# q and k of a transposed attention: seven products for eight, and a third of the depthwise taps on other engines

## The chip, the cores and the metric

The kernel runs on one core of a Trainium2 chip, in fp32 throughout. The metric is the device time of one execution in microseconds. The median of three runs of the kernel before is 2740.94 us (2740.43 to 2743.98).

## The reference, cut to what matters

The input x has 384 channels of 192 x 192 pixels. Layer 0 normalises it over groups of channels, makes q, k and v with a 1x1 convolution (384 to 1152 channels), pools 2x2 by the maximum, and applies a depthwise 3x3 convolution. q and k then only enter as their norms and as q k^T per head (48 x 48 a head), summed over all 96 x 96 pooled pixels. Layer 1 is a depthwise 7x7 convolution over the whole image.

```python
def _L0_conv_ref(x, w_qkv, b_qkv, w_dw, b_dw, w_proj, b_proj, temperature, a1, a2, a3, a4):
    ...
    qkv = jnp.einsum('bchw,oc->bohw', x, w_qkv) + b_qkv[None, :, None, None]
    hs, ws = (h // DS, w // DS)
    qkv = qkv.reshape(b, 3 * c, hs, DS, ws, DS).max(axis=(3, 5))
    qkv = lax.conv_general_dilated(qkv, w_dw, (1, 1), 'SAME', feature_group_count=3 * c, dimension_numbers=('NCHW', 'OIHW', 'NCHW'))
    qkv = qkv + b_dw[None, :, None, None]
    q, k, v = jnp.split(qkv, 3, axis=1)
    ...
    q = q / jnp.clip(jnp.linalg.norm(q, axis=-1, keepdims=True), 1e-12)
    k = k / jnp.clip(jnp.linalg.norm(k, axis=-1, keepdims=True), 1e-12)
    attn = jnp.einsum('bhcn,bhdn->bhcd', q, k) * temperature[None]
    ...
x = x + _L0_conv_ref(_gn(x), ...)
x = x + _L1_conv_ref(_gn(x), L1_conv_weight)
```

## The kernel before

The 384 channels lie on 128 partitions in three tiles (KT = 3); q and k together have six output tiles (ct = 0 to 5). The image is cut into 24 blocks (NB) of eight image rows, which are four pooled rows (PR) of 96 pixels (PS). The stages follow each other in this order:

- Statistics: x is read once; VectorE takes its moments. The first three blocks stay in on-chip memory (`held`), and as soon as two of the three channel tiles are normalised, TensorE begins the sums of blocks 0 and 1 (`begin`); ScalarE puts 20 of these begun sums aside (`spots`, in `rowbuf` and `more`).
- q and k, the stage that the change is in: a loop over b from 0 to 24. For each block and output tile, `pooled` runs three groups of 512 columns; a group is three matrix products (one a channel tile) into a bank of PSUM, and one VectorE reduction from there (L672), which takes the maximum of 2x2 and writes the pooled pixels into a `ring` of 14 rows per output tile. `bordered` copies the ring's wrap-around rows on ScalarE (L697, L701). One block later `depthwise` makes the nine taps of an output tile on VectorE (one scaled copy, L712, and eight multiply-adds, L717) into `qk`. `finish` turns the result in blocks of 32 x 32 on VectorE (L781), squares and sums it on ScalarE (L729), and after three output tiles 16 ScalarE copies (L735) finish the turning. `products` then adds 12 matrix products of the turned q and k to `grams` (L751), two blocks behind.
- v, the attention and the projection; then layer 1, whose matrices `weights` has meanwhile laid out on GpSimd (L578 to L605): one piece a block, from block 0 on.

The sums of q and k use a pool of four one-bank tiles of PSUM (`pq`), and a pool of three (`ptr`) takes small sums and the squares' unused output; `grams` has a bank of its own. The order of the instructions on an engine is mostly the program's own: from block 2 on `pinned` (and `keep`) hold each engine's instructions in the order in which they are written, and put gram products between the others.

An fp32 matrix product is two instructions on TensorE in the trace, each with a load of weights. The waits between engines are set by the recording layer from the tiles that the instructions read and write. The block of x is loaded by `load_x` on SyncE's queue into one of three buffers.

```python
    ptr = psx.enter_context(tc.tile_pool(name="ptr", bufs=3, space=PSUM))
    ...
    pq = qx.enter_context(tc.tile_pool(name="pq", bufs=4, space=PSUM))
    ...
                for kt in range(KT) if begun is None else (TWO,):
                    ins = nc.tensor.matmul(
                        ps,
                        wq[:, kt, ct * P : (ct + 1) * P],
                        rows[:, kt, :, g * 64 : (g + 1) * 64],
```

Of the kernel before, what the change touches and what calls it, by code (L numbers as in the profile page):

```python
# [13 lines left out]
P = 128  # L14
# [72 lines left out]
def conv_preact_d2(  # L87
# [184 lines left out]
    ptr = psx.enter_context(tc.tile_pool(name="ptr", bufs=3, space=PSUM))  # L272
    qx = ExitStack()
    pq = qx.enter_context(tc.tile_pool(name="pq", bufs=4, space=PSUM))
# [20 lines left out]
    with tc.tile_pool(name="stp", bufs=1) as stp, tc.tile_pool(name="xsp", bufs=5) as xsp:  # L295
# [29 lines left out]
        def total(name, n, terms):  # L325

            ps = ptr.tile([P, C], F32, name=name, tag="tr")
            for i, (lhs, rhs) in enumerate(terms):
                keep(
                    nc.tensor.matmul(  # L330
                        ps[:, 0:n], lhs, rhs, start=(i == 0), stop=(i == len(terms) - 1)
                    )
                )
            return ps[:, 0:n]
# [87 lines left out]
        def begin(i):  # L422
            b, ct, g = begun_qk[i]
            ps = pq.tile([P, 512], F32, name=f"pq{b}_{ct}_{g}_begun", tag="pq")
# [46 lines left out]
        bias_ps = ptr.tile([P, C], F32, name="bias_ps", tag="tr")  # L471
# [91 lines left out]
    with ExitStack() as bx:  # L563
# [6 lines left out]
        def weights(kt, i0, i1):  # L570
# [7 lines left out]
            nc.gpsimd.memset(g, 0.0)  # L578
            for kr in range(KS):
                lo, hi = max(i0, kr), min(i1, kr + TR)  # L580
                if lo < hi:
                    nc.gpsimd.tensor_copy(
                        bass.AP(
                            g.tensor,
                            g.offset + ((lo - i0) * GQ + CP - 1) * TR + lo - kr,
                            [g.ap[0], [TR, KS], [GQ * TR + 1, hi - lo]],
                        ),
                        w7s[:, kt, kr, :].unsqueeze(2).to_broadcast([P, KS, hi - lo]),
                    )
            lo, hi = max(i0, HALO), min(i1, HALO + TR)  # L590
            cs = slice(kt * P, (kt + 1) * P)
            for v in range(CP if lo < hi else 0):
                nc.gpsimd.dma_start(
# [6 lines left out]
                )  # L600
            for i in range(i0, i1):
# [3 lines left out]
                nc.gpsimd.dma_start(  # L605
# [6 lines left out]
                )  # L612
# [22 lines left out]
        ring = []  # L635
        for ct in range(2 * KT):
            ring.append(padp.tile([P, 3 * PR + 2, PS + 2], F32, name=f"ring{ct}"))
# [11 lines left out]
        def pooled(b, ct, xb, taps):  # L649
# [4 lines left out]
            for g in range(3):  # L654
                begun, there = sums_qk.pop((b, ct, g), (None, False))
                ps = begun
                if not there:
                    ps = pq.tile([P, 512], F32, name=f"pq{b}_{ct}_{g}", tag="pq")
# [44 lines left out]
        def depthwise(b, ct, dst, pin):  # L703

            r0 = b % 3 * PR
            for tap in range(9):
# [3 lines left out]
                if tap == 0:  # L710
                    pin(
                        nc.vector.tensor_scalar(  # L712
                            dst, src, w, bdb[:, ct : ct + 1], ALU.mult, ALU.add
                        )
                    )
                else:
                    pin(nc.vector.scalar_tensor_tensor(dst, src, w, dst, ALU.mult, ALU.add))  # L717
# [8 lines left out]
        def squares(b, ct, t):  # L726

            junk = ptr.tile([P, C], F32, name=f"junk{b}_{ct}", tag="tr")
            nc.scalar.activation(junk, t, AF.Square, accum_out=ssq[:, ct, b : b + 1])  # L729

        def turned(side, turns):

            for a in range(P // Q):
                for f in range(P // Q):
                    nc.scalar.copy(  # L735
                        side[f * Q : (f + 1) * Q].rearrange("p c (t n) -> p t c n", n=P)[
                            :, :, :, a * Q : (a + 1) * Q
                        ],
                        turns[a * Q : (a + 1) * Q].rearrange("p t (c n) -> p t c n", n=P)[
                            :, :, :, f * Q : (f + 1) * Q  # L740
                        ],
                    )
                yield
# [23 lines left out]
        copies, sides = iter(()), []  # L767
        turns = multiplied = None
# [4 lines left out]
        def finish(b, ct, dst, taps, now=False):  # L773

            nonlocal copies, turns
            some(taps, 9)
            s, t = divmod(ct, KT)
            if t == 0:
                turns = trp.tile([P, KT, PB], F32, name=f"turns{b}_{s}", tag=f"turns{s}")
            flat = dst.rearrange("p h w -> p (h w)")  # L780
            ins = nc.vector.transpose(turns[:, t], flat)  # L781
            if b > 0:
                pinned(ins)

            for _ in copies:
                pass
            squares(b, ct, flat)
            if t == KT - 1:
                side = trp.tile(
                    [P, PB // P, C], F32, name=f"qkT{b}_{s}", tag=f"qkT{s}", bufs=2 - s  # L790
                )
                sides.append(side)
                copies = turned(side, turns)
                for _ in range(4 if now else 2):
                    next(copies)
# [20 lines left out]

        last = None
        for b in range(NB + 1):
            xb, xvb = None, []
            if b < NB:  # L820
                xb = held.pop(b) if b in held else load_x(b, "xq")
            else:

                qx.close()
                pv = psx.enter_context(tc.tile_pool(name="pv", bufs=2, space=PSUM))
                for n in range(3):
                    t = xpool.tile([P, 2, UT, KT, RB * HW], F32, name=f"xv_begun{n}", tag="xb")
                    for k in range(2):
                        i, t0 = divmod((2 * n + k) * UT, NT)
                        for kt in range(KT):  # L830
                            nc.sync.dma_start(t[:, k, :, kt], image_rows(kt, order[i], t0, UT))
                        xvb += [(i, t0, ct, t[:, k]) for ct in range(KT)]
            for ct in range(2 * KT):
                dst, taps = None, iter(())
                if b > 0:
                    dst = qkp.tile([P, PR, PS], F32, name=f"qk{b}_{ct}", tag="qk")
                    taps = depthwise(b - 1, ct, dst, pinned if b > 1 else lambda ins: ins)
                if b < NB:
                    if ct == KT + 1 and b > 1:
                        done, sides = sides[0:2], sides[2:]  # L840
                        between.append(products(b - 2, done))
                    if b == 0 and ct < 2:

                        if ct == 0:
                            pooled(b, 0, xb, taps)
                            pooled(b, 1, xb, taps)
                            biases()
                    else:
                        pooled(b, ct, xb, taps)
                    bordered(b, ct)  # L850
# [5 lines left out]
                if b == NB:  # L856
                    if ct == KT - 1:
                        between.append(products(b - 2, sides[0:2]))
                    some(taps, 4)
                    convolve(*xvb.pop(0), pinned)  # L860
                    some(taps, 5)
                    convolve(*xvb.pop(0), pinned)
            if b == NB:
                finish(*last, True)
                for _ in range(2):
                    convolve(*xvb.pop(0), pinned)
                norms()
                for _ in products(b - 1, sides[2:4]):
                    pass
                for args in xvb:  # L870
                    convolve(*args, pe_keep)
            if b == 2:
                for tiles in vrows:
                    row_borders(tiles)
            if b < len(pieces):
                with tc.issue_after(stats0):
                    weights(*pieces[b])
# [793 lines left out]
```

## Time and profile before

| what | value |
|---|---|
| median of three runs | 2740.94 us |
| span of the profiled execution, first to last instruction | 2751.1 us |
| statistics, to the first product of block 0 | about 169.5 us |
| q and k, blocks 0 to 23 on TensorE | about 169.5 to 1302 us |
| last taps of q and k on VectorE | to about 1355 us |
| v, attention, projection, layer 1 | the rest |

The profile is of one execution, which took 10 us more than the median. Busy times of an engine are the union of its instructions; a group's line gives the sum and the mean of one. "Idle before" is the time in which the engine had nothing to run ahead of these instructions, and the name after it is what ended most of that.

### The profile page before, as it was taken

Reading aid. Unit: us, or ns where it says so; the run is one execution under the profiler, and the core shown is the slowest. Engines: PE = TensorE matmul, PEld = TensorE weight load, DVE = VectorE, ACT = ScalarE, POOL = GpSimd, SP = SyncE. Lnnn points to the kernel's source line nnn. Section 1 sums busy time; section 2 is a strip of 40 time slices with the busy share of each in tenths; the row PEclk is TensorE's granted clock in tenths of the full one; section 3 lists DMA queues with packets and bytes.
Section 4 is the critical chain, followed back from the end, with each engine's and each line's share of the span. In section 5 each row is a group of like instructions: output and inputs, shape, how many; then the busy total and the mean of one; then the engine's idle time right before and its main releaser. Section 6 shows DMA issues by size and latency. Waiting matters only on the chain. (4 is left out here: it accounts for less than half of the span.)

```text
span 2751.1 us, 25751 instructions
## 1 busy us (share of the span) xinstructions
PE 2583.4 (94%) x8365; PEld 1527.5 (56%) x8365; DVE 2404.7 (87%) x3538; ACT 1141.3 (41%) x2262; POOL 748.0 (27%) x885
## 2 busy tenths in 40 slices
PE   0399999999999999999989989999998999999998
PEld 0144444444444444444546656666666677777776
DVE  7989999999999999999898979988889788777886
ACT  0043334343334343333302322322324577777776
POOL 1024454100000000000002320100101577777887
PEclk9999999999999999999999999999999899999999
DMA  9976767401010110111136996675755999999998
GB/s 381 401 262 210 245 207 246 146 35 69 35 69 35 37 67 35 69 35 53 69 122 235 342 373 237 212 254 179 240 196 181 339 347 363 365 372 371 368 376 271
DMA packets 234087, 581.01 MB, mean 211 GB/s; under 512 B 16688, under 2 KB 165792, under 8 KB 217184
## 3 DMA queue, kind: packets, MB, share of 16 engines
q1 hardware_dynamic: 173456, 283.44, 29.4%
q0 software_dynamic: 37376, 148.85, 15.7%
q10 hardware_dynamic: 23120, 147.07, 14.2%
q8 instruction: 67, 1.10, 0.2%
q14 instruction: 68, 0.56, 0.1%
HBM read 370.93 MB, written 208.21 MB: 211 GB/s over the span
## 5 line engine op out<-in xcount | busy, mean ns | idle before, releaser
L662 PE MATMUL pq<-xq,wq 128*128 128x512 f32 x2268 | 1021.9, 595 | 0.0
L717 DVE SCALAR_TENSOR_TENSOR qk<-ring,wd,qk 128x384 f32<-128x384 f32 x1152 | 696.3, 615 | 25.1
L662 PEld LDWEIGHTS pq<-xq,wq 128*128 128x128 f32 x2268 | 411.7, 190 | 421.9 <-issue 372.4
L549 PE MATMUL pv<-xv,wq 128*128 128x384 f32 x1512 | 499.2, 490 | 18.1 <-DVE rows L555 9.5
L1575 PE MATMUL pc<-main,w 128*128 128x288 f32 x1536 | 435.0, 405 | 3.5 <-issue 1.3
L1595 DVE TENSOR_SCALAR apart<-pc,rb 32x576 f32<-32x576 f32 x384 | 312.2, 813 | 118.4 <-PE pc L1575 98.3
L549 PEld LDWEIGHTS pv<-xv,wq 128*128 128x128 f32 x1512 | 288.8, 192 | 220.2 <-DVE rows L555 13.2
L1575 PEld LDWEIGHTS pc<-main,w 128*128 128x128 f32 x1536 | 289.8, 189 | 86.8 <-issue 2.9
L1593 ACT ACTIVATE apart<-pc,rb 32x576 f32<-32x576 f32 x384 | 281.4, 733 | 132.8 <-PE pc L1575 128.0
L672 DVE TENSOR_REDUCE ring<-pq 128x128 f32<-128x512 f32 x428 | 290.0, 679 | 52.0 <-PE pq L662 51.2
L735 ACT COPY qkT<-turns 32x288 f32<-32x288 f32 x768 | 329.4, 429 | 12.1 <-DVE turns L781 3.2
L1041 DVE SCALAR_TENSOR_TENSOR vb<-rows,wd,vb 128x576 f32<-128x576 f32 x384 | 313.0, 818 | 10.8
L729 ACT ACTIVATE junk<-qk 128x384 f32<-128x384 f32 x144 | 71.2, 494 | 471.7 <-DVE qk L717 470.8
L1575 PE MATMUL pc<-aux,h 128*128 128x288 f32 x768 | 248.5, 405 | 1.1 <-POOL aux L1510 1.1
L803 POOL TENSOR_TENSOR rn<-rn,halfpos 128x6 f32<-128x6 f32 x1 | 1.4, 1359 | 842.7 <-DVE rn L802 842.7
L1534 POOL COPY res<-apart 128x1152 f32<-128x1152 f32 (+1 forms) x96 | 213.1, 2253 | 62.6 <-DMA out_dram<-res 51.2
L1168 DVE TENSOR_TENSOR sx<-xr,y 128x576 f32<-128x576 f32 x180 | 203.9, 1174 | 21.2 <-ACT y L1139 15.1
L1209 POOL DMA_DIRECT2D sd<-sx x96 | 72.2, 756 | 501.1 <-DVE sx L1168 482.2
L555 DVE TENSOR_REDUCE rows<-pv 128x192 f32<-128x768 f32 x144 | 137.8, 957 | 57.7 <-PE pv L549 57.7
L1575 PEld LDWEIGHTS pc<-aux,h 128*128 128x128 f32 x768 | 144.9, 189 | 42.9 <-POOL aux L1510 1.5
L751 PEld LDWEIGHTS grams<-qkT,qkT 128*96 128x96 f32 x576 | 92.1, 163 | 136.8 <-issue 132.1
L1188 ACT ACTIVATE wq<-sx,negmid 128x1152 f32<-128x1152 f32 x96 | 120.6, 1257 | 107.6 <-DVE sx L1168 103.4
(234 smaller groups left out, 2307.8 us busy)
## 6 DMA issues: line engine op xcount, KB each, us to landing
sd<-sx POOLq DMA_DIRECT2D x96, 600.0 KB, 10.0
out_dram<-res SPq DMA_DIRECT2D x192, 288.0 KB, 10.5
main<-sd ACTq DMA_DIRECT2D x46, 1200.0 KB, 7.0
xr<-in_x_dram SPq DMA_DIRECT2D x45, 1152.0 KB, 12.7
xq<-in_x_dram SPq DMA_DIRECT2D x21, 2304.0 KB, 8.1
xv<-in_x_dram SPq DMA_DIRECT2D x126, 384.0 KB, 6.4
w<-wt ACTq DMA_DIRECT2D x46, 1024.0 KB, 7.0
xs<-in_x_dram SPq DMA_DIRECT2D x24, 1536.0 KB, 15.1
```

What stands on the lines that cost most here:

```text
L549: nc.tensor.matmul(ps[:, u, 0 : RB * HW], wq[:, kt, o : o + P], xb[:, u, kt, :], start=(kt == 0), stop=(kt == KT - 1),)
L555: nc.vector.tensor_reduce(rows[ct][:, 1 + t0 : 1 + t0 + UT, 1 : PS + 1], ps[:, :, 0 : RB * HW].rearrange("p u (a w b) -> p u w a b", a=2, ...
L662: ins = nc.tensor.matmul(ps, wq[:, kt, ct * P : (ct + 1) * P], rows[:, kt, :, g * 64 : (g + 1) * 64], start=(kt == 0), stop=(kt == KT - 1) ...
L672: ins = nc.vector.tensor_reduce(t[:, r0 : r0 + PR, 1 + g * 32 : 1 + (g + 1) * 32], ps.rearrange("p (h a w b) -> p h w a b", h=PR, a=2, b=2 ...
L717: pin(nc.vector.scalar_tensor_tensor(dst, src, w, dst, ALU.mult, ALU.add))
L735: nc.scalar.copy(side[f * Q : (f + 1) * Q].rearrange("p c (t n) -> p t c n", n=P)[:, :, :, a * Q : (a + 1) * Q], turns[a * Q : (a + 1) * Q ...
L1041: pin(nc.vector.scalar_tensor_tensor(dst, src, w, dst, ALU.mult, ALU.add))
L1168: nc.vector.tensor_tensor(bass.AP(flat.tensor, flat.offset + at(e) + a * RUN, [flat.ap[0], [JP, NT], [1, NJ], [at(f) - at(e), 2]],), xq[:, ...
L1534: keep(copy(res[ps, k], apart[ps, :, k].rearrange("p e n -> p n e")))
L1575: nc.tensor.matmul(ahead[q][:, k, 0 : NT * NJ], lhs, rhs, start=(j == 0), stop=(j == 2), skip_group_check=True,)
L1593: keep(nc.scalar.mul(dst, src, scale))
L1595: keep(nc.vector.tensor_scalar_mul(dst, src, scale))
```

## The change

From block 2 on, the products over channel tiles 0 and 1 for a pair of output tiles are made by Strassen's scheme. The two output tiles and the two rows of a pooling pair form a 2 x 2 of blocks, and so do the two channel tiles; seven products of combined operands take the place of eight, and the third channel tile adds four as before. One such group covers a pair of output tiles and half of a block's columns: 384 columns of each operand, in 11 products; a block is six groups, all blocks 132.

- The combinations of weights (`combos`) are made once on GpSimd. The two channel tiles carry different normalisation factors, so `ratio` scales one to the other. The combinations of pixels (`mixes`: T4, T2, T1, T3) are made for each block and half by one ScalarE scaling of 768 columns (`prescaled`) and four GpSimd operations of 384 (`mixed`).
- The sums live in PSUM tiles of three banks: `bank_da` (D, and two banks that take the shared and base products in turn) and `bank_bc` (two banks B in turn, and C). ScalarE copies partial sums from bank to bank, four copies a group. VectorE makes one addition of 768 elements, one maximum of 768 and one of 384 a group, the last into the ring.
- Of the six output tiles' taps, tiles 0 and 3 (`MOVED`) go to `moved`: ScalarE multiplies, GpSimd adds. The other four stay on VectorE (`summed_up`), with their running sum in PSUM (`bank_r`).
- `turned` gives four of its 16 copies to GpSimd. `weights` is a generator now: its GpSimd steps for one block come in two portions in the block's second and third groups. The border rows of v's tiles (`row_borders`), done in block 2 before, come after the q/k stage, since their memory holds the mixes until then.
- All of this is in a fixed order, written out in the loop over groups; `some` and `fill_in` say how many taps, turning copies and squares go where.

```diff
-    ptr = psx.enter_context(tc.tile_pool(name="ptr", bufs=3, space=PSUM))
     qx = ExitStack()
-    pq = qx.enter_context(tc.tile_pool(name="pq", bufs=4, space=PSUM))
+    pb = qx.enter_context(tc.tile_pool(name="pb", bufs=1, space=PSUM))
+    bank_da = pb.tile([P, 3, 512], F32, name="bank_da")
+    bank_bc = pb.tile([P, 3, 512], F32, name="bank_bc")
+    bank_r = pb.tile([P, 512], F32, name="bank_r")
...
+    small = turns_of([bank_da[:, 1], bank_da[:, 2], bank_r])
+    large = turns_of([bank_bc[:, 0], bank_bc[:, 1], bank_bc[:, 2], bank_da[:, 0]])
...
-            ps = pq.tile([P, 512], F32, name=f"pq{b}_{ct}_{g}_begun", tag="pq")
+            ps = next(large)
...
+            acc = sum_bank(b)[:, 0:C].rearrange("p (r c) -> p r c", c=PS)
...
-                    pin(nc.vector.scalar_tensor_tensor(dst, src, w, dst, ALU.mult, ALU.add))
+                    into = dst if tap == 8 else acc
+                    pin(nc.vector.scalar_tensor_tensor(into, src, w, acc, ALU.mult, ALU.add))
...
+                    copy = nc.gpsimd.tensor_copy if a == f else nc.scalar.copy
...
+        def moved():
...
+                            keep(
+                                nc.scalar.mul(part.rearrange("p (h w) -> p h w", w=PS), src, w)
+                            )
+                            keep(nc.gpsimd.tensor_tensor(flat, flat, part, ALU.add))
...
+        def mixed(b, half):
...
+            keep(tt(t1, b12, b11, ALU.subtract))
+            keep(tt(t3, t2, b12, ALU.subtract))
+            yield
+            keep(tt(t2, t3, b11, ALU.add))
+            keep(tt(t4, t2, t4, ALU.subtract))
...
+        def bank_of(n):
+            return bank_da[:, 1 + n % 2]
+
+        def share(n):
+
+            b, pair, half = groups[n]
+            product(bank_of(n), combos[:, pair, 0], mixes[(2 * b + half) % 3][:, 2], True)
+            keep(nc.scalar.copy(shared5[n % 2], bank_of(n)[:, 0:HN]))
+
+        def base(n):
+
+            b, pair, half = groups[n]
+            product(bank_of(n), wq_of(0, 2 * pair), block_of(xbs[b], 0, 0, half), True)
+            keep(nc.scalar.copy(bank_bc[:, n % 2, 0:HN], bank_of(n)[:, 0:HN]))
+
+        def second(n):
+
+            b, pair, half = groups[n]
+            product(bank_of(n), wq_of(1, 2 * pair), block_of(xbs[b], 1, 0, half))
...
+            into_b, into_c, into_d = bank_bc[:, n % 2], bank_bc[:, 2], bank_da[:, 0]
+
+            product(into_b, s2, t2)
+            keep(nc.scalar.copy(into_c[:, 0:HN], into_b[:, 0:HN]))
+            some(grammed, 4)
+            product(bank_of(n), wq_of(2, one), block_of(xbs[b], 2, 0, half))
+            if begun:
+                some(apart, 1)
+            product(into_b, s3, t3)
+            keep(nc.scalar.copy(into_d[:, 0:HN], into_b[:, 0:HN]))
+            if more_to_come:
+                share(n + 1)
...
+            product(into_c, s4, block_of(xbs[b], 1, 1, half))
+            product(into_c, wq_of(2, one), block_of(xbs[b], 2, 1, half))
+            if begun:
+                some(apart, 1)
+            fill_in(3)
+            product(into_b, wq_of(2, two), block_of(xbs[b], 2, 1, half))
+            if more_to_come:
+                base(n + 1)
+            t = added[n % 2]
+            keep(
+                nc.vector.tensor_tensor(
+                    t,
+                    bank_bc[:, n % 2 : 3 : 2 - n % 2, 0:HN],
+                    shared5[n % 2].unsqueeze(1).to_broadcast([P, 2, HN]),
+                    ALU.add,
+                )
+            )
+            if begun:
+                some(taps, ahead[s])
+            product(into_d, a22, t4)
+            product(into_d, wq_of(2, two), block_of(xbs[b], 2, 0, half))
+            if b + 1 < NB and s in (3, 5):
+                prescaled(b + 1, int(s == 5))
+            if begun:
+                some(apart, 1)
+            fill_in(4)
...
+            if more_to_come:
+                second(n + 1)
+
+            keep(
+                nc.vector.tensor_tensor(
+                    t, bank_da[:, 0 : 2 + n % 2 : 1 + n % 2, 0:HN], t, ALU.max
+                )
+            )
...
+            if begun:
+                some(taps, behind[s])
...
+        for tiles in vrows:
+            row_borders(tiles)
```

`product` is one matrix product of 384 columns. Written out, TensorE's order in a group n is: S2·T2 into B; the third channel tile into the group's own bank of `bank_da`; S3·T3 into B; S1·T1 of group n + 1 (`share`); S4·B into C; the third tile into C; the third tile into B; the base product of group n + 1; A22·T4 into D; the third tile into D; the second product of group n + 1.

## The prediction

> **What bounds the kernel now.** I read the busy shares first, then the windows of the q/k stage, then the costliest groups of that stage, then single waits in order of time. The page's first lines, and its group lines for the stage:
>
> ```profile
> PE 2583.4 (94%) x8365; PEld 1527.5 (56%) x8365; DVE 2404.7 (87%) x3538; ACT 1141.3 (41%) x2262; POOL 748.0 (27%) x885
> ...
> L662 PE MATMUL pq<-xq,wq 128*128 128x512 f32 x2268 | 1021.9, 595 | 0.0
> L717 DVE SCALAR_TENSOR_TENSOR qk<-ring,wd,qk 128x384 f32<-128x384 f32 x1152 | 696.3, 615 | 25.1
> ```
>
> The window of blocks 3 to 23 (one block is four pooled rows of q and k):
>
> ```profile
> 278.00:1302.00 1024.00, 1023.86 (x2775) 473.88 (x2773) 950.28 (x1640) 389.56 (x1009) 105.68 (x165) 1.00 0.26 91
> ```
>
> The reader is to see that TensorE is never idle there, VectorE is at 93%, ScalarE at 38%, GpSimd at 10%. So 21 blocks take 1024 us, 48.7 us each. A block has 54 products of 512 columns, two instructions each; a row of 24 of them took 10.46 us and one lasts 0.59, so their pitch is 0.429: 108 x 0.429 = 46.3. The other 2.4 us are 12 gram products, 24 instructions at 0.10.
>
> Two spots show what a hand-over between engines costs:
>
> ```profile
> 704.61 1.05 PE L662 MATMUL pq<-xq,wq 128*128 128x512 f32 x2
> 705.70 0.69 DVE L672 TENSOR_REDUCE ring<-pq 128x128 f32<-128x512 f32 x1 [0.20 <-PE pq L662]
> ```
>
> ```profile
> 1301.90 0.69 DVE L672 TENSOR_REDUCE ring<-pq 128x128 f32<-128x512 f32 x1 [0.70 <-PE pq L662]
> 1302.64 0.91 PE L549 MATMUL pv<-xv_begun,wq 128*128 128x384 f32 x2 [0.79 <-DVE ring L672]
> ```
>
> A reader of a product starts 0.04 us after its recorded end, and that end lies 0.17 behind its pitch (0.49 against 0.32 for 384 columns). A product that waited starts 0.05 after its releaser, and the two then take 0.91 where 0.32 + 0.49 = 0.81 is their pace in a row: 0.10 is weights not loaded ahead. So a hand-over out of TensorE and back costs 0.17 + 0.04 + 0.05 + 0.10 = 0.36 us besides the other engine's own time.
>
> [...] VectorE reduces one pq bank while TensorE fills the next without a gap. [...]
>
> **The change part by part.** *Products.* From block 2 on a block is six groups (output pair, column half) of 11 products of 384 columns instead of 12. At a pitch of 0.322 for each instruction (24 pv instructions in 8.01 us) a group is 22 x 0.322 = 7.08; three groups a block carry 8 gram instructions, 0.82. A block is 6 x 7.08 + 2.4 = 44.9 against 48.7: 3.8 us less, if nothing waits.
>
> *Waits.* The list of what each instruction of the built program waits for decides the case. The pool of four one-bank tiles gives way to bank_da and bank_bc, tiles of three banks, and the waits are set per tile, not per bank. In all but the edge ones of the 132 groups TensorE's eleven products stand so (B, C, D are the banks of the sums):
> 1. S2·T2 into B waits for VectorE's add of the group before.
> 2. third tile, into its own bank, waits for VectorE's max (L1124 of the changed kernel) of the group before, though that read other banks. That max itself waits for product 11 of the group before.
> 3. S3·T3 into B waits for ScalarE's copy of B to C, which waits for product 1.
> 4. S1·T1 of the next group waits for the copy of B to D, which waits for product 3.
> 5, 6, 7 wait for nothing.
> 8. next group's base waits for the copy of product 4, three products back.
> 9. A22·T4 into D waits for the copy of the base, product 8, directly ahead of it.
> 10, 11 wait for nothing.
>
> So products 4 and 9 stand a whole round trip with nothing between. ScalarE's copy of 384 columns: L434 has 0.586 for 512, and a 96-column copy (L701) 0.273, 0.75 ns a column: 0.49. Each trip is 0.36 + 0.49 = 0.85, 1.70 a group. Product 2 waits from the end of product 11 for a max of 768 elements: the copy from PSUM of 384 (L233) took 0.557, so [...]0.95; 0.36 + 0.95 = 1.31, of which product 1 covers 0.64: 0.67 in groups without grams, nothing where 0.82 of grams stand there. The copy for product 3 (0.75 after product 1) hides behind product 2. A group is 7.08 + 1.70 + 0.67 = 9.45, with grams 7.08 + 0.82 + 1.70 = 9.60; a block 57.2.
>
> *ScalarE* gets four copies a group (2.0), three products (a 384-element one by a pointer scale took 0.60 at L492: 1.8), of the turning copies 24 of 32 a block at 0.44, six squares, two prescalings of 768 (0.93, L420): 6.5 us of a group of 9.5. Its queue is in order, and the base copy stands behind a product, a square and two turning copies, which end near 6.8 us of the group where the copy may start at 6.9. The square waits for VectorE's transpose behind four or five taps, up to 0.6 later. I take 0.2 a group, 1.2 a block; bounds 0 (all early) and 4 (0.6 to 0.7 in each).
>
> *GpSimd.* An add of 384: L179 has 0.472 for 147 elements, L182 0.237 for 21, 1.87 ns each, so 0.91[...]. Sixteen adds, eight mixings, eight turning copies (0.45) and the weights of the second layer (a memset 2.2, six copies at 0.32, four DMA issues at 0.83: 7.4) are 33 us of a block: no bound. The weights' steps, now in a block's second and third group, put at most 4 us ahead of an add; four part buffers, more than a group's, cover that for ScalarE. But T2 of a block's second half is made at the end of its first group, behind an add that waits for ScalarE and a turning copy: base copy ends at 7.5, product 8.05, add 9.0, copy 9.5, T2 10.45, where product 1 could go at 9.6. About 1.0 a block; a like late turning copy holds the grams, 0.3.
>
> *VectorE* loses 18 reductions (12.2) and two of six depthwise tiles; it gets two 768-element operations and one of 384 (0.55) a group, 2.45, or 14.7 a block, and four tiles of taps (22; sums in PSUM, which no row shows: 0.60 to 0.70 each, I take 0.62) and transposes 3.5: 40 of 59. It isn't the bound. Its two taps ahead of the max end as product 11 does.
>
> A block is 57.2 + 1.2 + 1.3 = 59.7, less 48.7 is 11.0; 22 blocks: **+242**.
>
> *Front.* The same tile waits hold the begun sums and blocks 0 and 1. Of 20 begun sums ten follow one in the same tile: 0.36 + 0.59 each, +9, and the third tile's mean at 159.8 stands behind them. Block 0's 20 chains (copy, product, reduction, 2.5 us) go one by one in a tile, some 14 in one: 35 us for 26. Block 1's 12 full sums, half of them at 0.36 + 0.68: +6. Together **+24**, bounds 5 and 45. The combinations of weights (GpSimd, 21 small operations) lie beside blocks 0 and 1.
>
> *Tail.* Block 23's last taps: 45 instead of 54 on VectorE at 0.62, less transposes moved: **-8**. The 45 border fills on ScalarE (15 us, L520) come after the q/k stage instead of in block 2; ScalarE idles for most of what follows, so nothing, at worst +10. The loads (8.1 us, three buffers, issued a block ahead) stay hidden.
>
> Sum: 242 + 24 - 8 = +258. The profiled execution's span of 2751.1 is 10 us above the median of 2740.9, which includes all that lies around it, so I put the difference on the median: **about 2999**.
>
> **The rivals.**
> *Waits cost nothing (faster).* If product 4, 9 and 2 found their releasers done, the stage runs at 44.9: 22 x -3.8 = -84, with front and tail 2741 - 84 + 16 = 2673. It decides once the stalls of a group sum to under 0.63 us (3.8 / 6). For it speaks that products 5 to 7 cover product 8's; against it that nothing stands between 3 and 4 or 8 and 9. 4%.
> *Waits, but shorter.* Copies at 0.40, weights loaded ahead (no 0.10), no late queue: a trip is 0.66, the max 0.50 exposed; group 8.9 and 9.2, block 54.4 + 0.5; 22 x 6.2 + 10 = +146: 2887. 14%.
> *ScalarE's queue becomes the bound.* Its 6.5 us are a third of a group short of it, but the copies sit in order behind products that need GpSimd's buffers; with 1 us late in each group a block is 65: 22 x 16.3 + 16 = +375: 3116. 12%.
> *Less is left out than it says.* The program holds 132 x 11 = 1452 products of the new form, so no.
>
> **How the numbers follow.** Forecast 70%, shorter waits 14%, late queue 12%, free waits 4%. Time 2999; the range from the shorter waits' 2887 to 3100, just short of the late queue, leaves under 2 in 10 out. A measurement here can tell some 0.2% from no change; faster 0.04, same 0.01, slower 0.95.
>
> **What would show it.** TensorE's busy share in the stage falling from 100% to some 78%; idle of about 0.6 us (from recorded end to start) ahead of A22·T4 and S1·T1, released by ScalarE's copies, 132 times each; some 0.4 ahead of the third tile's product, released by VectorE, in half the groups; a block of about 60 us by the loads of xq. Wrong, if products 4 and 9 start with no idle, if the copies take under 0.35, or if the stage's longest waits are on GpSimd.

## The result: 12.5% slower, and the profile after

The changed kernel takes 3087.25 us (median of 4 runs, 3079.86 to 3091.62) where the kernel before takes 2741.66 us beside it: a ratio of 1.1252, 95% interval 1.1224 to 1.128. The forecast was 2999 us, the range 2887 to 3100. The profiled execution has a span of 3078.1 us against 2751.1: 327 us more. Cut at the same marks in both traces, they lie in three places:

| part | before, us | after, us | difference | predicted |
|---|---|---|---|---|
| front, up to block 2's first products | 230.1 | 305.2 | +75 | +24 |
| stage, 22 blocks | 1072 | 1306 | +234 | +242 |
| tail | 1449 | 1467 | +18 | -8 |

The busy times of the changed kernel, from part 1 of its page, and the window of the stage (start and end in us, length, then busy us and instructions of TensorE, its weight loads, VectorE, ScalarE and GpSimd, the clock, DMA):

```profile
PE 2617.4 (85%) x8893; PEld 1603.3 (52%) x8893; DVE 2347.5 (76%) x3127; ACT 1563.2 (51%) x3056; POOL 1390.8 (45%) x1642
```

```profile
305.00:1611.00 1306.00, 1080.82 (x3403) 565.85 (x3401) 884.74 (x1297) 814.72 (x1827) 738.32 (x912) 1.00 0.23 83
```

TensorE was at 100% in this stage before and is now at 83%, at full clock; no other engine is above 68% (VectorE). A block takes 1306 / 22 = 59.4 us. (The prediction had 78%: it counted a product by its pitch, and the records after a wait run on by the 0.17 and 0.10 us of its hand-over sum, and 16 waits a block at 0.27 are the 4.2 us between 44.9 and the busy 49.1.) TensorE idles while no engine is full, so it waits for hand-overs; the list of TensorE's waits from 400 to 1600 us names them (total us, times, longest):

```profile
PE bank_da L1016 <- ACT bank_da L1078: 89.3, 121, 2.5
PE bank_da L1016 <- ACT bank_bc L1034: 69.3, 122, 0.6
PE bank_da L1016 <- DVE rows L1124: 24.7, 61, 0.4
PE bank_bc L1016 <- POOL rows L1011: 22.7, 20, 1.1
```

In 121 groups product 4 waits for the copy to D (L1078) and product 9 for the copy of the base (L1034), once each; in every second group product 2 waits for VectorE's maximum (L1124), and once a block product 1 waits for T2 (L1011). These are the four waits of the prediction, and there is no fifth of any size. One copy to D and one base copy in the timeline (start, us, engine, line; in brackets the idle before and its releaser):

```profile
958.42 0.81 PE L1016 MATMUL bank_bc<-rows,more 128*128 128x384 f32 x2
...
958.64 0.45 ACT L711 COPY ring<-ring 128x96 f32<-128x96 f32 x2 [0.58 <-DVE ring L1131]
958.99 0.61 ACT L874 ACTIVATE more<-ring,wd 128x384 f32<-128x384 f32 x1
...
959.51 0.47 ACT L1078 COPY bank_da<-bank_bc 128x384 f32<-128x384 f32 x1
960.12 0.88 PE L1016 MATMUL bank_da<-rows,more 128*128 128x384 f32 x2 [0.89 <-ACT bank_da L1078]
...
963.62 0.46 ACT L1034 COPY bank_bc<-bank_da 128x384 f32<-128x384 f32 x1 [0.22 <-PE bank_da L1016]
...
964.14 0.91 PE L1016 MATMUL bank_da<-rows,more 128*128 128x384 f32 x2 [0.55 <-ACT bank_bc L1034]
```

Product 3 ends at 959.23. ScalarE could copy at once, but two ring copies and a product are ahead of the copy to D in its queue, so it starts 0.28 us later than it could; product 4, which reads nothing of D, starts when it is done. The base copy at 963.62 is on time, and product 9 still stands 0.55 us: that is the bare round trip.

### The profile page after: what moved, and what is told of

It reads as the page before. It is cut to its first block, busy times and chain, and to the rows that moved or that the text cites. A ratio compares the mean times of both kernels' runs of the same rounds, so it can differ in the third digit from the quotient of the medians.

```text
span 3078.1 us, 28437 instructions
## 1 busy us (share of the span) xinstructions
PE 2617.4 (85%) x8893; PEld 1603.3 (52%) x8893; DVE 2347.5 (76%) x3127; ACT 1563.2 (51%) x3056; POOL 1390.8 (45%) x1642
## 5 line engine op out<-in xcount | busy, mean ns | idle before, releaser
L876 POOL TENSOR_TENSOR qk<-qk,more 128x384 f32<-128x384 f32 x368 | 366.7, 997 | 566.8 <-ACT more L874 557.9
L1016 PE MATMUL bank_da<-xq,wq 128*128 128x384 f32 x1008 | 395.9, 495 | 25.7 <-DVE rows L1124 25.5
L1095 DVE TENSOR_TENSOR rows<-bank_bc,rows 128x768 f32<-128x768 f32 x132 | 126.4, 958 | 368.7 <-ACT bank_bc L1034 365.4
L1016 PE MATMUL bank_da<-rows,more 128*128 128x384 f32 x528 | 240.3, 537 | 191.2 <-ACT bank_da L1078 94.9
L733 DVE SCALAR_TENSOR_TENSOR bank_r<-ring,wd,bank_r 128x384 f32<-128x384 f32 x623 | 386.4, 620 | 15.7
L1016 PEld LDWEIGHTS bank_da<-xq,wq 128*128 128x128 f32 x1008 | 180.5, 190 | 166.7 <-DVE rows L1124 64.2
L1016 PEld LDWEIGHTS bank_da<-rows,more 128*128 128x128 f32 x528 | 79.1, 189 | 352.4 <-ACT bank_bc L1034 127.3
L752 ACT COPY qkT<-turns 32x288 f32<-32x288 f32 x576 | 247.0, 429 | 8.6
L1016 PE MATMUL bank_bc<-rows,more 128*128 128x384 f32 x528 | 217.0, 493 | 23.8 <-POOL rows L1011 23.8
L874 ACT ACTIVATE more<-ring,wd 128x384 f32<-128x384 f32 x368 | 224.4, 613 | 8.0 <-POOL qk L876 3.6
```

The lines of the kernel that those rows point to most:

```text
L733: pin(nc.vector.scalar_tensor_tensor(into, src, w, acc, ALU.mult, ALU.add))
L752: copy(side[f * Q : (f + 1) * Q].rearrange("p c (t n) -> p t c n", n=P)[:, :, :, a * Q : (a + 1) * Q], turns[a * Q : (a + 1) * Q].rearrang ...
L874: nc.scalar.mul(part.rearrange("p (h w) -> p h w", w=PS), src, w)
L876: keep(nc.gpsimd.tensor_tensor(flat, flat, part, ALU.add))
L1016: nc.tensor.matmul(ps[:, 0:HN], lhs, rhs, start=start, stop=True, skip_group_check=True)
```

## The experiments

Every run was timed beside the kernel before on its own chip, where that kernel took 2752 to 2757 us, so kernels are compared by their ratio to it; expectations in us are for a kernel before of 2741. "Block" is the time from product 1 of block 2's first group to the first product of v, divided by 22; it was 48.8 us before and is 59.7 after (this count takes in the hand-over to v, the 59.4 above does not).

| run | ratio, 95% interval | block, us |
|---|---|---|
| one-bank tiles | 1.0382 (1.0365 to 1.0399) | 51.2 |
| split only | 1.1266 (1.125 to 1.1283) | 59.9 |
| D apart | 1.0788 (1.0766 to 1.081) | 54.8 |
| front earlier | 1.1213 (1.1185 to 1.124) | 59.7 |
| moved taps left out | 1.1042 (1.102 to 1.1063) | 57.4 |
| second part alone | 1.0324 (1.0302 to 1.0345) | 52.3 |
| the same, weights moved in the text | 1.0316 (1.0287 to 1.0346) | 52.3 |
| the same, their order held | 1.075 (1.0721 to 1.0778) | 49.0 |
| reordered | 1.0064 (1.0041 to 1.0087) | 47.7 |
| and tail | 1.0023 (1.001 to 1.0036) | 47.4 |
| and prescaling early | **0.9889** (0.9873 to 0.9905) | 46.0 |
| the last, sums in SBUF | 1.0507 (1.0488 to 1.0526) | 53.3 |

**One bank, one tile.**

```diff
-    bank_da = pb.tile([P, 3, 512], F32, name="bank_da")
-    bank_bc = pb.tile([P, 3, 512], F32, name="bank_bc")
+    bank_d, bank_a0, bank_a1, bank_b0, bank_b1, bank_c = [
+        pb.tile([P, 512], F32, name=f"bank_{k}") for k in ("d", "a0", "a1", "b0", "b1", "c")
+    ]
...
-                    t, bank_da[:, 0 : 2 + n % 2 : 1 + n % 2, 0:HN], t, ALU.max
+                nc.vector.tensor_tensor(t[:, 0], into_d[:, 0:HN], t[:, 0], ALU.max)
+            )
+            keep(
+                nc.vector.tensor_tensor(t[:, 1], bank_of(n)[:, 0:HN], t[:, 1], ALU.max)
```

> Every bank of the sums is a tile of its own; VectorE's add and max of two banks become two operations of one bank each. Theory (the stage waits because tiles of three banks are guarded whole): the waits ahead of product 4 (S1*T1) and product 2 (third tile) go, the wait of product 9 (A22*T4) becomes one of the product after next (second part of the next base) with 1.29 us of cover; what stays is the copy from B to C with product 2 alone as cover, some 0.2 us. A group 7.08 + half of 0.82 + 0.2 + late engines 0.2 = 7.9, a block 47 (46 to 51), stage 12 less a block, and the front's chains some 20 to 40 shorter: 2790 us (2740 to 2880). Rival (ScalarE's queue is the bound): copies stay late, the block stays over 56, time over 3000. Rival (the new products themselves are dearer than their pitch): about 3087.

2862.63 us, 1.0382 (2846 for a kernel before of 2741, within the band): of the changed kernel's 346 us over the kernel before, 106 are left. TensorE's waits from 400 to 1400 us in its trace:

```profile
PE bank_b L1017 <- POOL rows L1012: 40.8, 19, 2.2
PE grams L770 <- POOL qkT L753: 29.8, 19, 1.6
PE bank_b L1017 <- ACT bank_c L1073: 10.1, 19, 1.0
```

The waits ahead of products 4 and 9 and that for the maximum, over 180 us before, are gone (one of 0.8 us is left at the stage's end). ScalarE does the same operations in the same order, 8.5 us a block faster: its queue was not the bound. The begun sums and blocks 0 and 1 came back too: block 0 began at 169.7 us and block 1's products ended at 228.6, against 169.5 and 230.2 before. The block was expected at 47 (46 to 51) and takes 51.2; it stays higher because T2 and the turning copy ahead of the grams, both GpSimd's, are late in 19 blocks of 19. Behind the wait of 2.15 us for T2 there are slow products in some blocks: at 1026.14 us the two take 1.59; at 1281.43 they take 0.91, as behind the shorter waits, but the grams behind them 1.44 for 0.84; at 1231.31 all keep their pace. The first of these blocks, and after the dots the last:

```profile
1023.18 0.81 PE L1017 MATMUL bank_a<-xq,wq 128*128 128x384 f32 x2
1026.14 1.59 PE L1017 MATMUL bank_b<-rows,more 128*128 128x384 f32 x2 [2.15 <-POOL rows L1012]
1027.52 1.49 PE L770 MATMUL grams<-qkT,qkT 128*96 128x96 f32 x8
1028.80 1.26 PE L1017 MATMUL bank_a<-xq,wq 128*128 128x384 f32 x2
1029.89 0.81 PE L1017 MATMUL bank_b<-rows,more 128*128 128x384 f32 x2
...
1231.31 0.91 PE L1017 MATMUL bank_b<-rows,more 128*128 128x384 f32 x2 [2.15 <-POOL rows L1012]
1232.06 0.84 PE L770 MATMUL grams<-qkT,qkT 128*96 128x96 f32 x8
1232.74 0.84 PE L1017 MATMUL bank_a<-xq,wq 128*128 128x384 f32 x2
1233.41 0.81 PE L1017 MATMUL bank_b<-rows,more 128*128 128x384 f32 x2
```

**The split without the banks.** The tiles of three are kept.

```diff
-                    t, bank_da[:, 0 : 2 + n % 2 : 1 + n % 2, 0:HN], t, ALU.max
+                nc.vector.tensor_tensor(t[:, 0], into_d[:, 0:HN], t[:, 0], ALU.max)
...
+                nc.vector.tensor_tensor(t[:, 1], bank_of(n)[:, 0:HN], t[:, 1], ALU.max)
```

> Tiles of three banks stay; only VectorE's add and max are split into two operations of 384, as the one-bank version needs. Theory of whole tiles: no gain, product 2 waits for two operations of about 0.62 instead of one of 0.96, up to 0.3 more in half of 132 groups: 3087 to 3115 us. If the split itself were what helps the one-bank version (shorter holds of each bank): under 3070.

3105.26 us, 1.1266, within the interval of the changed kernel's ratio: the split alone gives nothing, and the four waits of 400 to 1600 us are still there (86.9, 69.4, 28.6 and 22.7 us). What the first experiment gained is the guarding of the banks.

**D apart.** Only D is a tile of its own, and only the maximum is split.

```diff
+    bank_d = pb.tile([P, 512], F32, name="bank_d")
+    bank_a = pb.tile([P, 2, 512], F32, name="bank_a")
     bank_bc = pb.tile([P, 3, 512], F32, name="bank_bc")
```

> Only bank D leaves its tile of three; the two own banks stay one tile, and B and C stay another; the max is split. Theory of whole tiles: the waits of products 4 and 9 go (0.74 and 0.57 us of idle each in the trace, 1.3 a group, 132 groups: -173), product 2 waits for both maxima, up to +0.3 in half the groups (+20): about 2935 us (2890 to 2980). Rival (ScalarE's queue): the copies come no earlier and the idle moves to the next product that needs one: over 3030.

2973.65 us, 1.0788 (2957 for a kernel before of 2741, within the band). The waits of products 4 and 9 are gone, and what was hidden behind them came out (400 to 1400 us):

```profile
PE bank_a L1017 <- DVE rows L1128: 67.3, 73, 1.2
PE bank_bc L1017 <- POOL rows L1012: 37.1, 19, 2.0
PE grams L770 <- POOL qkT L753: 21.0, 18, 1.2
```

Product 2's wait for the two maxima is 0.92 us now, not 0.4 + 0.3. Removing two waits that sum to 1.3 us in a group freed 0.82 (4.9 a block over 6): a wait also covers what is late behind it.

**The front earlier.** The ratio is formed behind the begun sums, the combinations and first mixings are issued after block 1's second output tile.

```diff
                 bordered(b, ct)
+                if (b, ct) == (1, 1):
+                    mixing = combined()
```

> The ratio of the scales is formed right behind the begun sums, and the 21 combinations of weights with block 2's first mixes of pixels are issued after block 1's second output tile instead of after block 1. Theory (PE's hole of 21 us before block 2 is GpSimd's combinations behind VectorE's ratio): the hole and the slow-clock products behind it go, -18 to -27: about 3065 us. Rival (the hole is the end of block 0's taps and block 1's chains, which the first group waits for too): -5 or less, over 3080.

3091.51 us, 1.1213; the intervals of this ratio and the changed kernel's just overlap, so about 10 us came of it, and perhaps none, where 18 to 27 were expected. The hole, in the changed kernel (first two lines) one wait, is two in this one:

```profile
276.31 1.88 PE L676 MATMUL bank_da<-xs,wq 128*128 128x512 f32 x4
...
299.35 1.65 PE L1016 MATMUL bank_da<-rows,more 128*128 128x384 f32 x2 [21.16 <-POOL rows L1008]
```

```profile
276.84 1.88 PE L681 MATMUL bank_da<-xs,wq 128*128 128x512 f32 x4
285.37 1.62 PE L969 MATMUL bank_da<-rows,more 128*128 128x384 f32 x2 [6.65 <-DVE qk L738]
292.38 1.65 PE L969 MATMUL bank_da<-xs,wq 128*128 128x384 f32 x2 [5.39 <-ACT rows L981]
```

Both theories hold in part. GpSimd no longer decides, and the first group starts 9 us earlier in the span (296.0 for 305.2). But block 0's last taps (VectorE, sums in the same tile) and the 12 turning copies of block 0 on ScalarE are the next to end.

**ScalarE's load.**

```diff
-                        else:
+                        elif False:
                             part = parts[k % len(parts)]
```

> The changed kernel; of the two moved depthwise tiles of blocks 1 to 23 only the first tap is computed, their other eight products (ScalarE) and sums (GpSimd) are left out, 9.8 and 16 us a block. Theory of whole tiles: the round trips ahead of products 4 and 9 stay, only what is late on ScalarE (1.2 us a block in the prediction) and GpSimd (1.0 to 1.3) goes: 1 to 2.5 us a block, -22 to -55 from the changed kernel, ratio to the kernel before 1.105 to 1.118. Rival (ScalarE's queue is the bound): 8 to 9.8 us a block, ratio under 1.06.

3044.32 us, 1.1042, just below the band. In its trace, from 400 to 1500 us, the wait for D is 68.0 us in 116 groups (0.59 each, 0.74 after), that for the base 65.8 in 116 (0.57, as after), and T2 is not in the list. A block is 2.3 us shorter although 9.8 us of ScalarE's work and 16 of GpSimd's (the counts of the expectation) went: what is late, not what is busy, was worth time.

**The second part alone,** on the kernel before:

```diff
+                    if b > 1 and ct in (0, KT):
+                        taps = apart(b - 1, ct, dst)
```

> The kernel before, with only the second part of the change: of blocks 1 to 23, two of six depthwise tiles as nine ScalarE operations and eight GpSimd sums, the convolution as it was. Theory: in the stage TensorE is at 100%, so taking 18 x 0.615 us of VectorE's 48.7 us a block buys nothing and 18 x 0.62 us more on ScalarE (38% to 61%) costs nothing: ratio to the kernel before 0.997 to 1.006. Rival (GpSimd's sums slow VectorE's reductions and taps while both read SBUF, or the chains of the moved tiles end late): 1.008 to 1.02.

2846.71 us, 1.0324: 91 us slower, and outside what either theory allowed. The stage ends at 1381.0 us instead of 1302.6, and TensorE waits 61 us for VectorE's reductions. One of these waits:

```profile
510.89 2.18 POOL L578 MEMSET g<- 128x2496 f32 x1 [3.08 <-DMA wt<-g]
513.13 1.14 POOL L582 COPY g<-w7s 128x14 f32<-128x14 f32 x7
514.99 0.91 POOL L593 DMA_DIRECT2D wt<-g  x1 [0.73 <-POOL g L582]
515.92 1.00 POOL L838 TENSOR_TENSOR qk<-qk,more 128x384 f32<-128x384 f32 x1
...
519.58 1.00 POOL L838 TENSOR_TENSOR qk<-qk,more 128x384 f32<-128x384 f32 x1
...
520.62 0.58 DVE L781 STREAM_TRANSPOSE turns<-qk 128x384 f32<-128x384 f32 x1 [18.71 <-POOL qk L838]
521.12 0.65 DVE L672 TENSOR_REDUCE ring<-pq 128x128 f32<-128x512 f32 x1
...
521.83 3.78 PE L662 MATMUL pq<-xq,wq 128*128 128x512 f32 x4 [13.22 <-DVE ring L672]
```

Read from the bottom: TensorE has filled its four banks and waits for a reduction; that stands behind the transpose of a moved tile; the transpose waits 18.71 us for the tile's last sum; and GpSimd, before that sum, laid out a piece of the second layer's weights, which waited for a DMA. VectorE's taps are also dearer, 0.739 us in the mean instead of 0.616 (its reductions are not: 0.674 for 0.678), so there were two candidates. The first try at telling them apart put the pieces behind the stage in the program's text:

```diff
-            if b < len(pieces):
+            if b < 2 or b == NB:
                 with tc.issue_after(stats0):
-                    weights(*pieces[b])
+                    for piece in pieces[b : b + 1] if b < 2 else pieces[2:]:
+                        weights(*piece)
```

> The second part alone again, with the second layer's weights of all pieces but two moved on GpSimd from the q/k stage to its end. Theory (the moved tiles' sums stand in GpSimd's queue behind those pieces and their DMAs, VectorE's transpose of a moved tile stands behind the sums, the reductions behind the transpose, TensorE behind the reductions): the waits of TensorE for reductions, 61 us in the trace of the second part alone, nearly go within the stage, which ends 50 to 75 us earlier; if nothing waits for the pieces after it, ratio to the kernel before 1.003 to 1.015. Rival (operands in SBUF, VectorE's taps 0.74 instead of 0.62 us, are the cause): stage as long as it was, ratio over 1.025.

2845.78 us, 1.0316, the same as before it: the planner of the recording layer, which places the instructions whose order the program does not hold, had put the pieces back into the stage (one of them is in the trace at 384.8 us). This run says nothing on either theory. The second try held their order:

```diff
-            nc.gpsimd.memset(g, 0.0)
+            keep(nc.gpsimd.memset(g, 0.0))
```

> As the run before, with the weights' GpSimd instructions and DMA issues held to the program's order, so that the pieces from the third on do come after the q/k stage on GpSimd's queue (in the run before the planner had put them back where they were). Theory (the moved tiles' sums stand behind the pieces): TensorE's 61 us of waits for reductions nearly go and the stage ends 50 to 75 us earlier than the 1381 us of the second part alone. What the 16 or so pieces cost after the stage, where they now stand in one row of about 8 us each, may be anything from nothing to 80 us, so the stage decides, not the total. Rival (operands in SBUF, VectorE's taps 0.74 us): the stage ends within 15 us of 1381.

The stage ends at 1306.6 us, 4 us after that of the kernel before, though a tap still takes 0.741. TensorE's waits for reductions in the stage (total us, times, longest), in the second part alone and with the pieces held behind:

```profile
PE pq L662 <- DVE ring L672: 61.4, 15, 13.2
```

```profile
PE pq L662 <- DVE ring L672: 4.7, 6, 0.8
```

So the queue on GpSimd was the cause, and the dearer taps cost next to nothing there, since VectorE was at 81% (809.58 of 1000 us from 300). (The total is 2960.71 us, 1.075: with the pieces in a row on GpSimd, VectorE waits for it 139 us, and TensorE for VectorE 146 us, in one wait in v.) In the stage, the second part as such costs next to nothing, given an order that keeps GpSimd's sums clear of the pieces; it gains nothing either.

**Towards a version that pays.** On the one-bank version with the front of the fourth run, T2 and T4 of the second half are made at the end of the block before, and the grams one group later:

```diff
                 next(mixing, None)
+                if s == 5:
+                    next(mixing, None)
...
-            some(grammed, 4)
+            some(grammed, 4 if s > 0 else 0)
```

> One-bank tiles as in the first experiment, the front as in the fourth, and two steps moved: GpSimd makes T2 and T4 of a block's second half at the end of the block before instead of in the block's first group, and the gram products stand in the block's second to fourth group instead of first to third. Theory: of the one-bank version's 50.7 us a block, the wait for T2 (2.15, with some 1.5 of slow TensorE behind it) and that for the turning copy ahead of the grams (1.57) go: 46 us a block, -95, front -8 to -20: ratio to the kernel before 0.99 to 1.01. Rival (GpSimd's queue, 65% busy there, hands the wait to the next step): block over 49, ratio over 1.02.

2774.77 us, 1.0064; both waits are gone. GpSimd handed part of them on, though: a wait for T1 of 1.2 us, once a block, has come in their place (23.5 us in 20 blocks), and the block takes 47.7 us where 46 were expected. Then the end of the stage:

```diff
-    bank_r = pb.tile([P, 512], F32, name="bank_r")
+    pr = psx.enter_context(tc.tile_pool(name="pr", bufs=1, space=PSUM))
+    bank_r = pr.tile([P, 512], F32, name="bank_r")
...
-                if len(sides.get(bb, ())) == 2 and bb == NB - 2:
+                if len(sides.get(bb, ())) == 2 and bb == NB - 2 and k > 2:
```

> The version before it, with two edits where the q/k stage ends: the bank of the taps' sums keeps its own pool, so that the banks of the pv products are free when the last maximum has read (8.1 us of TensorE idle), and the gram products of block 22 come three convolutions later (9.6 us of idle). Theory: 12 to 20 us less than the version before it, ratio to the kernel before 0.984 to 1.004. Rival (both gaps are filled from time that is lost anyway further on): within 4 us of it.

2761.73 us, 1.0023: 13 us less; the wait for banks fell from 8.1 to 1.2 us, that of the grams from 9.6 to 3.5. Then the order on ScalarE:

```diff
                 share(n + 1)
+            if b + 1 < NB and s in (3, 5):
+                prescaled(b + 1, int(s == 5))
```

> The version before it, with the prescaling of the next block's pixels behind the copy to D in the fourth and sixth group (it stood ahead of the copy to C), the first half of the sixth group's mixing right behind it, and the first group's three products ahead of block 0's last transpose and turning copies. Theory: the two waits left in a block of 47.4 us (1.2 for T1, 0.5 for the late copy to C) go, block 45.8, and 8 to 14 us of the front's idle: -44 to -50 us: ratio to the kernel before 0.984 (0.978 to 0.992), the first version under it. Rival (VectorE, 85% busy there, or ScalarE's queue is next): block over 47, ratio over 0.995.

2722.65 us against 2752.33 beside it, 0.9889: 1.1% less, and the only version here that is faster than both kernels. The wait for T1 is gone; that for the copy to C stayed (12.4 us in 15 waits; the version before had 11.8 in 23). From 241.22 to 1240 us:

```profile
241.22:1240.00 998.78, 986.84 (x3378) 580.77 (x3377) 868.80 (x1548) 801.86 (x1810) 719.11 (x899) 1.00 0.30 109
```

TensorE is at 99% again; a block takes 46.0 us, near the 44.9 that the prediction counted for products without waits, and 2.8 under the 48.8 before. Of the 61 us that 22 such blocks save, 25 reach the end of the profiled execution: 9 are lost ahead of block 2, which begins at 238.9 us, and 27 behind the stage (11 in v's first 108 products, those on `xv_begun`, and 14 from there to v's last); what holds v up was not sought. Last, the same version with VectorE's running sums in SBUF:

```diff
-            acc = sum_bank(b)[:, 0:C].rearrange("p (r c) -> p r c", c=PS)
+            acc = dst if b > 0 else sum_bank(b)[:, 0:C].rearrange("p (r c) -> p r c", c=PS)
```

> The version with the early prescaling, but the running sum of VectorE's taps from block 1 on in SBUF, as in the kernel before the change, instead of in a PSUM bank. Theory (two operands in SBUF on VectorE and on GpSimd at a time hold each other up): taps of 0.62 grow to about 1.0 in the mean, 36 of them add some 14 us to VectorE's 40 us a block, which becomes the bound: block 52 to 57, ratio to the kernel before 1.03 to 1.08, and GpSimd's sums lengthen too. Rival (the place of the sum is nothing to either engine): within 0.5% of the version with the early prescaling.

2892.55 us, 1.0507. The groups of VectorE's taps from 300 to 1200 us (count, busy us, mean ns, idle before), with the sums in PSUM and in SBUF:

```profile
L741 DVE SCALAR_TENSOR_TENSOR bank_r<-ring,wd,bank_r 128x384 f32<-128x384 f32 x549 | 339.9, 619 | 14.8
```

```profile
L741 DVE SCALAR_TENSOR_TENSOR qk<-ring,wd,qk 128x384 f32<-128x384 f32 x537 | 488.2, 909 | 14.5
```

A tap grows from 0.62 to 0.91 us, GpSimd's sum of a moved tile from 1.00 to 1.09, and VectorE is at 92% and has become the bound: from 300 to 1300 us TensorE waits 80.9 us for ScalarE's copy of the base, and ScalarE, in whose queue these copies stand, waits 104.1 us for VectorE's transposes. The place of the sum alone is not what is dear: in the kernel before it lay in SBUF too, and a tap took 0.616 with GpSimd 9% busy; with the weights behind, 0.741 at 36%; here 0.909 at 72%. With the sum in the PSUM bank that the change gives to the taps it was 0.619 with GpSimd at 74%.

## Why the prediction was right, and where it was not

*The stage was right, sum and mechanism:* 59.4 us a block for 59.7. Its terms: the bare round trip was put at 0.85, which is an idle of 0.58 plus 0.27 of pitch tail and weights; the base's wait shows 0.57. The maximum was put at 0.67 in half of the groups: 0.40 of idle plus 0.27, in 61 of 121. ScalarE's delay has the right size and the wrong place: 1.2 a block were expected ahead of product 9, behind a square and turning copies; it came ahead of product 4, behind ring copies and a product, (0.74 - 0.57) x 6 = 1.0. T2 was 1.4 a block (1.1 of idle and 0.27) for 1.0, with GpSimd's add at 1.00 us for 0.91. VectorE's operation on 768 elements was put at 0.95, an estimate (in the trace before, a reduction of 768, L555, took 0.956 in the mean), and took 0.96. The 0.3 for late grams did not show. That these waits come from guarding whole tiles is shown by the first three runs: without it they vanish, with the split alone they stay.

*The front was wrong by 51 us,* and its +75 lies outside the bounds of 5 and 45, in two steps.
- "The combinations of weights (GpSimd, 21 small operations) lie beside blocks 0 and 1." They do not. They take 11.0 us on GpSimd, from 287.3 to 298.3, after block 1's products ended at 278.2. They wait for `ratio` at 285.2 on VectorE, whose queue first has to end block 0's taps and transposes, and the first mixing comes behind them. TensorE stood 21.2 us and then ran slowly (the granted clock was 0.50 from 299 to 305 us, and two instructions took 1.65 for 0.91), +27 in all. The mistake was to place them by their data (the weights are ready early) and not by their position in the order of the program. The fourth run adds that freeing GpSimd alone would have been worth about 10: ScalarE and VectorE end soon after.
- Blocks 0 and 1 were put at +9 and +6 and took +38. A chain (copy, product, reduction) was put at 2.5 us at full clock. In the trace:

```profile
227.55 2.08 PE L676 MATMUL bank_bc<-xs,wq 128*128 128x512 f32 x2 [1.41 <-ACT bank_bc L674]
231.03 2.08 PE L676 MATMUL bank_bc<-xs,wq 128*128 128x512 f32 x2 [1.41 <-ACT bank_bc L674]
```

3.48 us each: TensorE, idle for 1.4 us of each, ran its products at half the clock (2.08 for two, with a granted clock of 0.50 from 225 to 235 us; 1.12 from 221 to 224, with 1.00). Over both blocks it waits 21.1 us where it waited 1.8, which is near the +15 of the prediction, and it is busy 77.7 us where it was busy some 59 with the same products. The term that was mis-sized is the product's own time in a chain with waits, about 19 us. The begun sums, +10 for +9, were right.

*The tail had the wrong sign,* +18 for -8 (+2 with the border fills at worst). The taps left at its start were counted, and two hand-overs were not: v's first product waits 7.9 us, because the bank of the tap sums is released only when VectorE's last tap of the tile is done, and the grams of block 22 wait 9.6 us for ScalarE's turning copies:

```profile
PE grams L769 <- ACT qkT L752: 9.6, 1, 9.6
PE pv L561 <- issue: 7.9, 1, 7.9
```

The run "and tail" took 13 us of this away. These two waits are 17.5 of the 28 us by which the stretch from the stage's end through v's first 108 products (those on `xv_begun`) has grown, from 78 to 106 us; from there to v's last product it takes 10 us less than before, which nothing here explains.

*The sum.* Stage -8, front +51 and tail +26 against their terms make +69 on the span. The remaining 19 of the 88 between 2999 and 3087 is the profiled execution: 10 above its median before, 9 under it after. That 3087 still lies within the range, 13 us from its end, is luck as far as the front and the tail go: the range's upper end was set by a late ScalarE queue, which did not come.

*The rivals.* ScalarE's queue as the bound falls with the first run and the one that leaves the moved taps out. The shorter waits fall too: the two copies shown took 0.46 and 0.47 us, not 0.40, and product 9 stood 0.57 us, the forecast's own 0.58. That waits cost nothing was wrong for this kernel, but it is what the reordered versions approach: the arithmetic saving is there, 2.8 us a block, and it takes one-bank tiles and several changes of order to see it.

## What to carry to other kernels

In this kernel a saving in products on a full engine was only had once nothing new stood between them. So list for every product what it waits for, as the built program has it, and count how many products lie between the releaser's start and the wait. Give each bank a tile of its own where banks are read and written by turns; one instruction over two banks saves little (0.96 us against twice 0.55). Place small preparations by their position in every queue they pass, and after each wait that is removed look for the next one; here those for T2, for the turning copy, for T1 and for the copy to C came out in turn.

## What the runs showed of the hardware that was not expected

- *VectorE and GpSimd on SBUF.* In the version with early prescaling a tap with its sum in PSUM took 0.62 us with GpSimd 74% busy; with the sum in SBUF it took 0.91 in the mean at 72%, and GpSimd's sum of a moved tile 1.09 for 1.00. A maximum of two SBUF operands at 957.30 in the changed kernel, begun 0.11 us after one of GpSimd's mixing steps, took 1.30 us; the one at 967.37, begun 0.12 us ahead of a step, took 0.56, and then the step took 1.30, where the shortest of the 44 on its line (L1012) took 0.99.
- *TensorE's clock after short waits.* In the changed kernel waits of 1.4 us, repeated every 3.5 us, went with half the clock (two products 2.08 for 1.12, granted clock 0.50 from 225 to 235 us), though the pair at 221.57, after a wait of 1.41, still took 1.12 at a granted clock of 1.00. In the one-bank version a wait of 2.15 us, 9.4 us behind one of about 1.6, was followed by slow instructions at 1026.14 and 1281.43 and by none at 1231.31. With D apart four waits of 1.95 us (at 1222.75, 1277.02, 1386.54 and 1441.22), 9.4 us behind one of 1.08 to 1.18, were followed by none: 0.91 us for two. What followed was longer by 0.96 us a pair in the chains, and by 1.65 in all at 1026.14 (3.75 us to the product at 1029.89, 2.10 for the same stretch from 1231.31). No length of wait from which it happens can be read from these runs.
